# Two levels of seven products for the second pass's queries, over pairs of groups and both blocks

## The chip, the core and the metric

The kernel runs on one core of a Trainium2 chip. The metric is the time of one execution in device microseconds (us). The engines are PE (TensorE matmul; PEld is its load of weights), DVE (VectorE), ACT (ScalarE), POOL (GpSimd) and SP (SyncE, which here only issues DMAs). Each engine works its instructions off in the order of the program. Matmuls write PSUM; DVE and ACT read PSUM, POOL works on tiles in SBUF alone.

## What is computed

Two layers are applied to x of 8 x 256 tokens with 1024 channels, everything in float32:

```python
# layer 0: autocorrelation of layernorm(x) against ctx, times tanh(gate); then a linear layer with a
#          low-rank part whose rank is chosen by token
# layer 1, attention (the part that the change touches):
q = (layernorm(x) @ wq).reshape(B, S, 32, 128)     # 32 query heads
k = (ctx @ wk).reshape(B, S, 8, 128)               # 8 key heads, each serves a group of 4 query heads
v = (ctx @ wv).reshape(B, S, 8, 128)
q, k = rope(q), rope(k)
x = x + tanh(g) * (softmax(mask(q @ k.T / sqrt(128))) @ v) @ wo
# layer 1, a linear layer with folded low-rank parts
```

## The kernel before, in words

The 2048 tokens are worked off in two passes of 1024 tokens (`p` = 0, 1). Each pass has four stages, one after the other: `autocorrelation` with the keys and values beside it, `lora_ffn`, `attention`, `fourier_ffn`. A pass keeps its tokens in eight tiles `xt` of 128 tokens; four of them are a block, so a pass has two blocks of 512 tokens.

Nearly all large matrix products are done with seven products in place of eight (a 2 x 2 scheme of Strassen and Winograd): `left_operands` (L206) and `right_operands` (L215) make three sums and a difference of an operand's quarters, the products run in the order SEVEN = (1, 2, 6, 7, 4, 5, 3), and `combine` (L223) or `add_product` (L247) puts them together on DVE as they come. Stored sums of weights are written to memory in the first pass and loaded later.

`attention` goes over steps, one for each (block, group): all eight groups of block 0, then those of block 1. For a step:

- `load_wq` brings the seven operands of the group's query weights (512 KB each) two steps ahead, and `queries` (L967 to L978) runs seven products of 2 x 4 matmuls with 256 columns. `combine` takes seven DVE instructions for them. The four finished quarters, which still lie in PSUM, go through `rope` (L709 to L717): three DVE instructions and an add on POOL (L717). The scratch tile of `rope` has one buffer.
- `query_operands` makes the block's seven right-hand operands: a normalisation on DVE, 32 transposes on PE, copies on ACT, four sums on DVE. For block 0 this happens at the end of `lora_ffn`, for block 1 at step 6.
- `scores` is called four times a step, `values` one call behind. A score call is four matmuls (L1131), then masking and the maximum on DVE, exp and scaling on ACT; a value call is eight transposes (L1166) and four matmuls (L1177).
- The output projection follows. In the second pass (`paired`) it takes two steps together, `outputs_of_two` (L1015 onwards), in two levels of seven: 49 products of two matmuls with 256 columns (L1067). Its weights are streamed by `stream_wo`, seven tiles ahead; sums of the outer level's left operand are made on POOL (L1046, L1056, L1116, L1119). The first pass has written its finer weights with `finer_weights` (POOL, L921 to L924).

The queries and the projection are generators. Two tables in the code, `q_fill` and `o_fill`, say how many of their products are put around each of a step's four score calls, so that PE has work while DVE and ACT do the softmax. A scheduler then sets the final order of the instructions on each engine. Query products and output products share four PSUM buffers (`at_mm`), scores have two, transposes and values two. Every DMA is issued by SP, in order; an issue waits until its destination tile is free. The large tiles come from rings of seven buffers for each of three groups: the tiles of the normalised x ("xn"), `gq` and `go`.

Of the kernel before, what the change touches and what calls it, by code (L numbers as in the profile page):

```python
# [11 lines left out]
F32 = mybir.dt.float32  # L12
# [7 lines left out]
P = 128  # L20
# [26 lines left out]
def flamingo_kernel(ctx: ExitStack, tc: tile.TileContext, a: dict, out: bass.AP):  # L47
# [52 lines left out]


    wo2_d = [dram.tile([P, 7, 2, 2, 2, S], F32, name=f"wo2_d{i}") for i in range(N_KV // 2)]

    wk_d, wv_d = (
        [[dram.tile([P, KC * P], F32, name=f"{k}_d{u}_{i}") for i in range(4)] for u in range(2)]
# [3 lines left out]
    def big_tile(group, shape, name):  # L109
        return big.tile([P, *shape], F32, tag=group, name=name)  # L110
# [229 lines left out]
    def norm_stats(tiles):  # L340
# [10 lines left out]
        nc.vector.reciprocal(rstd[:, :n], rstd[:, :n])  # L351
        return mv, rstd

    def normed(dst, xt, mv, rstd, i):
        nc.vector.tensor_scalar(
            dst, xt, mv[:, i, 0:1], rstd[:, i : i + 1], ALU.subtract, ALU.mult
        )
# [25 lines left out]
    def autocorrelation(p, xt, pools, beside, late):  # L383
# [11 lines left out]

        def normalize(b0, b1):

            n = b1 - b0
            mv, rstd = norm_stats(xt[b0 * 2 : b1 * 2])
            lin = stats.tile([P, 2 * n, 2], F32, tag="lin", name="lin", bufs=2)  # L400
            nc.vector.tensor_copy(lin[:, :, 0], rstd[:, : 2 * n])
            nc.vector.scalar_tensor_tensor(
                lin[:, :, 1], mv[:, : 2 * n, 0], -1.0, rstd[:, : 2 * n], ALU.mult, ALU.mult
            )
            for b in range(n):
                norms[b0 + b] = lin[:, b * 2, :], lin[:, b * 2 + 1, :]

        def dft(*terms):
# [438 lines left out]

    def attention(p, xt, gq, go, keep, norms, xops, ahead):  # L850
        with (
            tc.tile_pool(name="at1", bufs=1, reuse_waits="tile") as w1,
# [5 lines left out]
            steps = [(blk, g) for blk in range(TT // NBT) for g in range(N_KV)]  # L858
            wq, wo, kv = {}, {}, {}
            paired = p == NPASS - 1  # L860

            def load_wq(step):
                blk, g = step
                if p == 0 and blk == 0:
                    q = [
                        [big_tile(gq, [2, KH, DH], f"wq_{i}{k}") for k in range(2)]
                        for i in range(2)
                    ]
                    for i, k in ((0, 0), (0, 1), (1, 0), (1, 1)):
                        nc.sync.dma_start(q[i][k], a["wq"][g, i, k])  # L870
                    s = [big_tile(gq, [2, KH, DH], f"wq_s{i}") for i in (1, 2, 4)]
                    ops = left_operands(nc.vector, q, *s)
                    for d, r in zip(wq_d[g], (5, 7, 6, 3)):
                        nc.sync.dma_start(d, ops[r])
                else:
                    ops = {}
                    where = {1: a["wq"][g, 0, 0], 2: a["wq"][g, 0, 1], 4: a["wq"][g, 1, 1]}
                    where |= dict(zip((5, 7, 6, 3), wq_d[g]))
                    for r in SEVEN:
                        ops[r] = big_tile(gq, [2, KH, DH], f"wq_{r}")  # L880
                        nc.sync.dma_start(ops[r], where[r])
                wq[step] = ops

            def load_wo(step):
                blk, g = step
# [43 lines left out]
            def stream_wo():  # L929

                places = []
                for _, g in steps[::2]:
                    for n, r in enumerate(SEVEN):
                        q = [
                            [wo_operand(g + k, r)[:, :, j * S : (j + 1) * S] for j in range(2)]
                            for k in range(2)
                        ]
                        d = wo2_d[g // 2][:, n]
                        places += [(q[0][0], q[1][0]), d[:, 0], d[:, 1], (q[1][1],)]
                tiles = []  # L940
                for n, src in enumerate(places):
                    for coming in places[len(tiles) : n + 7]:
                        tiles.append(big_tile(go, [2, 2, S], "wo"))
                        if isinstance(coming, tuple):
                            for i, part in enumerate(coming):
                                nc.sync.dma_start(tiles[-1][:, i], part)
                        else:
                            nc.sync.dma_start(tiles[-1], coming)
                    for i in range(len(src) if isinstance(src, tuple) else 2):
                        yield tiles[n][:, i]  # L950
# [16 lines left out]
            def queries(step, qT):  # L967

                wops, xo = wq[step], xops[step[0]]
                tiles = {}  # L970
                for r in SEVEN:
                    ps = ps_mm.tile([P, 2, S], F32, tag="mm", name="ps_q")
                    for l in range(2):
                        for c in range(KH):
                            nc.tensor.matmul(  # L975
                                ps[:, l, :],
                                wops[r][:, l, c, :],
                                xo[r][:, c, :],  # L978
                                start=(c == 0),
                                stop=(c == KH - 1),  # L980
                            )
                    done = combine(r, ps, tiles, lambda tag: half(tag, 1), lambda ps: ps)
                    if done:
                        qT[done[1]] = half("qT", 7)
                        rope(qT[done[1]], done[0], tab_q[:, 0, :], tab_q[:, 1, :], w1)
                    yield

            def outputs(step, ops):
                blk = step[0]
# [199 lines left out]
                    next(gen, None)  # L1189

            nothing = iter(())
            fine = nothing
            new_xl = lambda: big_tile("xn", [D], "xl")
            if paired:
                wo_stream = stream_wo()
            load_wq(steps[0])
            load_kv(steps[0])
            qT = {}
            for _ in queries(steps[0], qT):
                pass  # L1200
            norms[1] = norm_stats(xt[NBT:])
            load_wq(steps[1])
            last, before, o_gen = [], None, nothing
            end = len(steps) - 1

            if paired:
                q_fill = {0: (2, 2, 1, 1), 1: (2, 2, 2, 1), end: (0, 0, 0, 0)}
                o_fill = {k: (0, 5, 10, 10) if k % 2 == 0 else (3, 5, 8, 8) for k in range(end)}
                o_fill[end] = (6, 6, 6, 6)
            else:  # L1210
                q_fill = {0: (2, 2, 1, 1), end: (0, 0, 0, 0)}
                o_fill = {k: (0, 1, 3, 3) for k in range(end)}
                o_fill[end] = (2, 2, 2, 1)
            middle = 4 if paired else 1

            def start_outputs():
                if paired:
                    got = outputs_of_two(last[0][0][0], [oT for _, oT in last])
                else:
                    s = [half(f"oS{j}", 1) for j in (1, 2, 4)]  # L1220
# [3 lines left out]

            oT = [[None, None], [None, None]]
            for k, step in enumerate(steps):
                follow = k + 1 < len(steps)
                following = {}
                if follow:
                    load_kv(steps[k + 1])  # L1230
                    q_gen = queries(steps[k + 1], following)
                    if k == 0:
                        fill_from(q_gen, 1)
                else:
                    q_gen = nothing
                for i, (n, l) in enumerate(((0, 0), (0, 1), (1, 0), (1, 1))):
                    got = scores(step, l, n, qT)
                    nq = q_fill.get(k, (3, 3, 1, 0))[i]
                    no = o_fill[k][i]
                    fill_from(q_gen, nq)  # L1240
                    mid = min(no, middle)
                    if i > 0:
                        fill_from(o_gen, no - mid)
                    if before is not None:
                        values(*before, lambda: fill_from(o_gen, mid))
                    before = step, l, n, got, oT
                    if i == 0:
                        if len(last) == 1 + paired:
# [1 line left out]
                            fill_from(o_gen, no)  # L1250
                        else:
                            fill_from(o_gen, no - mid)
                    if i == 2 and k + 2 < len(steps):
                        if steps[k + 2][1] == 0:
                            blk = steps[k + 2][0]
                            xb = xt[blk * NBT : (blk + 1) * NBT]
# [3 lines left out]
                        load_wo(step)  # L1260
                    if i == 0 and p == 0 and step[0] > 0 and step[1] % 2:
                        fine = finer_weights(step)
                    fill_from(fine, 1)
                for _ in q_gen:
                    pass
                if not paired or k % 2:
                    for _ in o_gen:
                        pass
                last.append((step, oT))
                oT = [[None, None], [None, None]]  # L1270
                qT = following
            values(*before, lambda: None)
            o_gen = start_outputs()
            fill_from(o_gen, 14 if paired else 2)
# [73 lines left out]
    for p in range(NPASS):  # L1348
# [42 lines left out]
        with tc.tile_pool(name="at_keep", bufs=1, reuse_waits="tile") as kp:  # L1391
            keep, norms, xops = [], {}, {}

            def before_attention(pool, ps_t, tag):
                norms[0] = norm_stats(xt[:NBT])
                new = lambda: pool.tile([P, D], F32, tag="xn", name="xl")
                xops[0] = query_operands(xt[:NBT], norms[0], new, ps_t, tag)
                for b in range(BP):
                    mf = pool.tile([P, 2, S], F32, tag="mf", name="mf")
                    nc.sync.dma_start(mf, a["mask"][p * BP + b].rearrange("(i p) k -> p i k", p=P))  # L1400
# [171 lines left out]
```

## Time and profile before

Three runs took 3330.26, 3332.24 and 3340.0 us. The profiled execution was a fourth:

| | |
|---|---|
| its own time | 3340.92 us |
| span, first to last instruction | 3339.1 us |
| granted TensorE clock, mean | 0.992 |
| PE idle, whole span | 72 us |
| second pass's attention begins (first query) | 2212.9 us |
| its last score call | about 3175 us |
| matmuls of the queries, both passes (ps_q, L975) | 3584 records |
| memory traffic | 505.55 MB, 151 GB/s |
| longest wait for POOL by PE (before L1004, first pass's end) | 6.02 us |

The profile gives for each group of instructions its line, engine, operation, output and inputs, size, count, busy time and mean. A matmul of float32 appears as two records. Views by stage give the busy time of each engine in a stretch of the span. A view of waits gives who waited for whom; the chain goes back from the last instruction to what released it. "Idle before" is the time for which an engine stood still ahead of an instruction, with the instruction that ended it.

### The profile page before, as it was taken

Reading aid. Unit: us, or ns where it says so; the run is one execution under the profiler, and the core shown is the slowest. Engines: PE = TensorE matmul, PEld = TensorE weight load, DVE = VectorE, ACT = ScalarE, POOL = GpSimd, SP = SyncE. Lnnn points to the kernel's source line nnn. Section 1 sums busy time; section 2 is a strip of 40 time slices with the busy share of each in tenths; the row PEclk is TensorE's granted clock in tenths of the full one; section 3 lists DMA queues with packets and bytes.
Section 4 is the critical chain, followed back from the end, with each engine's and each line's share of the span. In section 5 each row is a group of like instructions: output and inputs, shape, how many; then the busy total and the mean of one; then the engine's idle time right before and its main releaser. Section 6 shows DMA issues by size and latency. Waiting matters only on the chain. (4 is left out here: it accounts for less than half of the span.)

```text
span 3339.1 us, 39371 instructions
## 1 busy us (share of the span) xinstructions
PE 3267.4 (98%) x13456; PEld 2405.0 (72%) x13456; DVE 2221.3 (67%) x4305; ACT 1051.6 (31%) x2555; POOL 1404.9 (42%) x1181
## 2 busy tenths in 40 slices
PE   8999899999999999999999999999999999999999
PEld 6677456777677777775456677568888888888874
DVE  7787657777776655565647686456666767666773
ACT  1332111433333433334113332115343434334420
POOL 4554111323332474576344442112454454454572
PEclk9999999999999999999999999999999999999999
DMA  7534615333433354554354435043555455555551
GB/s 280 175 115 125 235 65 186 130 134 129 145 124 130 132 208 145 183 195 162 115 190 130 138 117 171 7 158 101 168 175 167 160 167 172 166 168 176 171 192 51
DMA packets 215781, 505.55 MB, mean 151 GB/s; under 512 B 25076, under 2 KB 102900, under 8 KB 215582
## 3 DMA queue, kind: packets, MB, share of 16 engines
q1 hardware_dynamic: 214430, 498.84, 44.2%
q0 software_dynamic: 1152, 4.19, 0.3%
q8 instruction: 108, 1.77, 0.2%
q14 instruction: 91, 0.75, 0.1%
HBM read 394.96 MB, written 108.00 MB: 151 GB/s over the span
## 5 line engine op out<-in xcount | busy, mean ns | idle before, releaser
L717 POOL TENSOR_TENSOR qT<-qT,rope 128x512 f32<-128x512 f32 x128 | 170.1, 1329 | 789.9 <-DVE qT L716 750.8
L975 PE MATMUL ps_q<-xn,wq 128*128 128x256 f32 x1920 | 428.9, 379 | 0.0
L975 PEld LDWEIGHTS ps_q<-xn,wq 128*128 128x128 f32 x1920 | 364.8, 190 | 50.5 <-PE po L677 0.5
L1145 ACT ACTIVATE s<-s,nmx 128x256 f32<-128x256 f32 x512 | 255.9, 500 | 245.0 <-DVE nmx L1142 244.8
L1140 DVE COPY_PREDICATED s<-keep,ps_s 128x512 f32<-128x512 uint8 x256 | 184.8, 727 | 156.0 <-PE ps_s L1131 155.1
L975 PE MATMUL ps_q<-xn_t,wq 128*128 128x256 f32 x1280 | 285.6, 379 | 0.0
L370 DVE SCALAR_TENSOR_TENSOR x<-po,tg,x 128x512 f32<-128x512 f32 x248 | 177.3, 743 | 139.3 <-PE po L1319 44.7
L975 PEld LDWEIGHTS ps_q<-xn_t,wq 128*128 128x128 f32 x1280 | 243.2, 190 | 33.1
L1172 ACT COPY wT<-pt 128x512 f32<-128x512 f32 x256 | 138.8, 586 | 361.8 <-PE pt L1166 361.8
L1131 PE MATMUL ps_s<-kT,qT 128*128 128x256 f32 x1024 | 247.9, 379 | 0.0
L1177 PE MATMUL av<-wT,v 128*128 128x256 f32 x1024 | 246.0, 382 | 1.7 <-ACT wT L1172 1.6
L1154 ACT ACTIVATE s<-s,tot 128x256 f32<-128x256 f32 x512 | 230.1, 497 | 40.6 <-DVE tot L1152 40.5
L1177 PEld LDWEIGHTS av<-wT,v 128*128 128x128 f32 x1024 | 191.4, 190 | 54.8 <-issue 22.2
L1067 PE MATMUL po<-wo,oI 128*128 128x256 f32 x896 | 214.7, 379 | 2.0 <-issue 1.2
L1131 PEld LDWEIGHTS ps_s<-kT,qT 128*128 128x128 f32 x1024 | 191.8, 190 | 25.1 <-issue 0.5
L1004 PE MATMUL po<-wo,oT 128*128 128x512 f32 x448 | 201.6, 593 | 0.0
L1067 PEld LDWEIGHTS po<-wo,oI 128*128 128x128 f32 x896 | 168.7, 190 | 25.6 <-issue 2.0
L1185 ACT COPY oT<-av 128x512 f32<-128x512 f32 x128 | 75.0, 586 | 353.9 <-PE av L1177 352.4
L1142 DVE TENSOR_REDUCE nmx<-s 128x2 f32<-128x512 f32 x256 | 173.2, 682 | 6.9
L1067 PE MATMUL po<-wo,oT 128*128 128x256 f32 x672 | 172.1, 382 | 1.9 <-DVE co L1082 0.3
L253 POOL TENSOR_TENSOR x<-x,part 128x512 f32<-128x512 f32 x48 | 68.3, 1423 | 247.1 <-ACT part L252 247.1
L1004 PEld LDWEIGHTS po<-wo,oT 128*128 128x128 f32 x448 | 83.0, 191 | 83.2 <-issue 74.8
(290 smaller groups left out, 6407.1 us busy)
## 6 DMA issues: line engine op xcount, KB each, us to landing
wo<-wo_d SPq DMA_DIRECT2D x144, 512.0 KB, 4.6
wq<-in_wq_dram SPq DMA_DIRECT2D x104, 512.0 KB, 3.5
wq<-wq_d SPq DMA_DIRECT2D x96, 512.0 KB, 3.3
wo<-in_wo_dram SPq DMA_DIRECT2D x56, 512.0 KB, 3.5
wo_d<-fine_t SPq DMA_DIRECT2D x56, 512.0 KB, 3.4
wo<-wo_d SPq DMA_DIRECT2D x96, 256.0 KB, 3.4
w<-w_d SPq DMA_DIRECT2D x36, 512.0 KB, 5.3
wo<-in_wo_dram SPq DMA_DIRECT2D x72, 256.0 KB, 3.3
```

Source lines behind the costliest of these rows:

```text
L370: nc.vector.scalar_tensor_tensor(xs, ps, g, xs, ALU.mult, ALU.add)
L717: nc.gpsimd.tensor_add(dst, dst, t)
L975: nc.tensor.matmul(ps[:, l, :], wops[r][:, l, c, :], xo[r][:, c, :], start=(c == 0), stop=(c == KH - 1),)
L1004: nc.tensor.matmul(po, ops[r][:, h, t * P : (t + 1) * P], wops[r][:, h, :], start=(h == 0), stop=(h == 1),)
L1067: nc.tensor.matmul(po, left[r2][:, h, :], w[:, h, :], start=(h == 0), stop=(h == 1))
L1131: nc.tensor.matmul(ps[:, t, :], qT[i, n][:, l, t * P : (t + 1) * P], kT[:, n * S : (n + 1) * S], start=True, stop=True,)
L1140: nc.vector.copy_predicated(s, keep[b], ps)
L1142: nc.vector.tensor_reduce(nmx, s, AX.X, ALU.max, negate=True)
L1145: nc.scalar.activation(s[:, t, :], s[:, t, :], AF.Exp, bias=nmx[:, t : t + 1], accum_out=tot[:, t : t + 1],)
L1154: nc.scalar.activation(s[:, t, :], s[:, t, :], AF.Copy, scale=tot[:, t : t + 1])
L1172: nc.scalar.copy(wT[i], pt)
L1177: nc.tensor.matmul(av[:, i, :], kv[step][1][:, n * 2 + c, :], wT[i][:, c, :], start=(c == 0), stop=(c == 1),)
```

## The change

Only the queries of the second pass change in what is computed how; a step of preparation is added to the first pass.

**Second pass.** Seven products remain the inner level (`n`), and a second level of seven (`r1`) is laid over them. Its left operand is the weights of two groups, split by group and by half of the inner contraction; its right operand is the inner operands of both blocks. So all queries of two groups and two blocks, four steps, come from 49 products of 2 x 2 matmuls with 256 columns (`queries_of_all`), one generator for all pairs of groups. Each outer product is first combined from its seven inner ones, then its four quarters are combined among the outer ones by further DVE instructions; finished quarters go through `rope` as before.

The steps are in another order: for each pair of groups (block 0, g), (0, g+1), (1, g+1), (1, g). Both operands of a product are streamed by `load`, 256 KB each, seven products ahead. For the first two outer products (`m < 14`) the right operand is block 0's own tile.

`second_block` makes block 1's operands at the start of the attention rather than at step 6: normalisation on ACT, transposes on PE, copies on ACT, four sums on DVE, and then for the outer level 28 subtractions of 128x512 on POOL, whose results SP writes to memory (`x2_d`), where `load` fetches them. It runs beside the first 14 products.

**First pass.** `finer_queries` loads the inner operands of two groups, makes the four outer sums on POOL (4 x 7 subtractions or additions of 128x512 for each pair of groups, 112 in all) and writes them to memory (`wq2_d`). It runs beside block 0's steps, one part at each score call.

The tables `q_fill` and `o_fill` of the second pass are new, and one query product of each call is moved between the transposes and the matmuls of `values`.

In the built program PE has 7392 instructions where it had 7504, DVE 4310 (4113), ACT 2040 (2019), POOL 1319 (1179) and SP 1653 (1128).

```diff
+            if paired:
+                order = (0, 0), (0, 1), (1, 1), (1, 0)
+                steps = [(blk, g + i) for g in range(0, N_KV, 2) for blk, i in order]
...
+            def finer_queries(g):
...
+                coming = [load(0)[0]]
+                yield
+                for n in range(7):
+                    (q00, q01), (q10, q11) = coming[n]
+                    if n < 6:
+                        coming.append(load(n + 1)[0])
+                    nc.gpsimd.tensor_add(q11, q10, q11)
+                    nc.gpsimd.tensor_sub(q10, q00, q10)
+                    nc.gpsimd.tensor_sub(q00, q11, q00)
+                    nc.gpsimd.tensor_sub(q01, q01, q00)
+                    for i, q in enumerate((q00, q01, q10, q11)):
+                        nc.sync.dma_start(
+                            wq2_d[g // 2][:, n, i], q.rearrange("p l d -> p (l d)")
+                        )
+                    yield
...
+            def second_block(kept):
...
+                for u in range(4):
+                    norm(u)
+                    turned(u)
+                yield
+                lin.append(factors(xt[NBT + 2 : TT]))
+                norm(4)
+                norm(5)
+                yield
+                yield
+                for u in range(4, 8):
+                    if u % 2 == 0 and u < 6:
+                        norm(u + 2)
+                        norm(u + 3)
+                    turned(u)
+                    if u % 2:
+                        yield
+                sums = Steps(nc.vector)
+                s = [big_tile(go, [KH, S], f"xn_t{i}") for i in (1, 2, 4)]
+                ops = right_operands(sums, q, *s)
+                late = {}
+                for n, r in enumerate(SEVEN):
+                    if n < 4:
+                        sums.run((0, 2, 1, 3)[n])
+                    both = xops[0][r], ops[r]
+                    b = [x[:, k * KQ : (k + 1) * KQ, :] for k in range(2) for x in both]
+                    t1, t2 = (half("oT", 13) for _ in range(2))
+                    nc.gpsimd.tensor_sub(t1, b[1], b[0])
+                    nc.gpsimd.tensor_sub(t2, b[3], t1)
+                    flat = [t.rearrange("p b s -> p (b s)") for t in (t1, t2)]
+                    nc.sync.dma_start(x2_d[n][3][:, 0], flat[1])
+                    nc.sync.dma_start(x2_d[n][2][:, 0], flat[0])
+                    late[n] = b, t2
+                    kept[0] += 1
+                    yield
+                for n, r in enumerate(SEVEN):
+                    b, t2 = late[n]
+                    nc.gpsimd.tensor_sub(b[1], b[3], b[1])
+                    nc.sync.dma_start(x2_d[n][1], ops[r].rearrange("p (k c) s -> p k (c s)", k=2))
+                    nc.gpsimd.tensor_sub(t2, t2, b[2])
+                    nc.sync.dma_start(x2_d[n][4][:, 0], t2.rearrange("p b s -> p (b s)"))
...
+            def queries_of_all(kept, qT, places):
...
+                            while len(ops) < min(m + 7, kept[0]):
+                                load()
+                            w = ops[m][:, 0].rearrange("p (l c d) -> p l c d", l=2, c=KQ)
+                            if m < 14:
+                                k = m // 7
+                                x = xops[0][r][:, k * KQ : (k + 1) * KQ, :]
+                            else:
+                                x = ops[m][:, 1].rearrange("p (c s) -> p c s", c=KQ)
+                            m += 1
+                            ps = ps_mm.tile([P, 2, S], F32, tag="mm", name="ps_q")
+                            for l in range(2):
+                                for c in range(KQ):
+                                    nc.tensor.matmul(
+                                        ps[:, l, :],
+                                        w[:, l, c, :],
+                                        x[:, c, :],
+                                        start=(c == 0),
+                                        stop=(c == KQ - 1),
+                                    )
+                            at = {2: (0, 0), 5: (1, 1), 3: (0, 1), 4: (1, 0)}.get(r)
+                            dest = lambda ps: u1[at] if r1 == 1 else ps
+                            done = combine(r, ps, tiles, lambda tag: half(tag, 1), dest)
+                            if done and r1 != 1:
+                                u, w = u1[at], w1_[at] if r1 in (7, 4, 5) else None
+                                if r1 == 7:
+                                    nc.vector.tensor_add(w, ps, u)
+                                if r1 in (6, 5):
+                                    nc.vector.tensor_add(u, ps, u)
+                                if r1 == 4:
+                                    nc.vector.tensor_sub(ps, w, ps)
+                                if r1 in (2, 5, 3):
+                                    nc.vector.tensor_add(ps, ps, w if r1 == 5 else u)
+                                if r1 in (2, 4, 5, 3):
+                                    step = {2: (0, g), 4: (0, g + 1), 5: (1, g + 1), 3: (1, g)}[r1]
+                                    q = next(places["q"])
+                                    rope(q, ps, tab_q[:, 0, :], tab_q[:, 1, :], w1)
+                                    qT.setdefault(step, {})[at] = q
+                            yield
...
+                sums = second_block(kept)
+                next(sums)
+                for _ in range(14):
+                    next(q_gen)
+                    next(sums)
+                for _ in sums:
+                    pass
...
+                q_fill = {k: (3 + (k % 4 == 1), 3, 3, 3) for k in range(end)}
+                q_fill[0] = 6, 6, 6, 6
+                q_fill |= {end - 2: (2, 2, 2, 1), end - 1: (1, 1, 1, 1), end: (0, 0, 0, 0)}
+                o_fill = {k: (4, 7, 7, 7) if k % 2 == 0 else (6, 6, 6, 6) for k in range(end + 1)}
...
+                    late = paired and nq > 0
+                    fill_from(q_gen, nq - late)
+                    mid = min(no, middle - 2 * late)
```

## The prediction, made before the changed kernel had run

> **What bounds the kernel now.** I read the busy rows of the page first, then the busy time by stage, then the chain.
>
> ```profile
> PE 3267.4 (98%) x13456; PEld 2405.0 (72%) x13456; DVE 2221.3 (67%) x4305; ACT 1051.6 (31%) x2555; POOL 1404.9 (42%) x1181
> ```
>
> PE is busy for 98%, so only less PE work can bring much. By stage (us; busy time and instructions of PE, PEld, DVE, ACT, POOL; granted clock; DMA share; GB/s):
>
> ```profile
> 520.00:1000.00 480.00, 479.12 (x1958) 349.01 (x1957) 355.40 (x536) 168.43 (x446) 150.53 (x108) 1.00 0.41 145
> ...
> 2213.00:2340.00 127.00, 126.98 (x618) 110.61 (x617) 82.72 (x149) 54.68 (x150) 27.21 (x25) 1.00 0.37 120
> ...
> 2730.00:2860.00 130.00, 129.76 (x633) 113.68 (x631) 92.95 (x181) 51.94 (x136) 61.33 (x60) 1.00 0.52 170
> ```
>
> The second pass's attention begins at 2213. PE idles there for 0.24 us in 130, DVE has about 30% free, POOL half. Its opening, 2213 to 2340, has no idle PE at all. The chain, in order of time, is PE's own instructions:
>
> ```profile
> 2213.02 27.63 PE ps_q L975 x128
> 2242.38 6.91 PE ps_q L975 x32
> ```
>
> Those 128 records last 27.63 us: 0.2159 us a record, and an f32 matmul of 256 columns is two records (the program has 1792 such query matmuls, the page's L975 groups 3584 records), so 0.4317 us.
>
> **The saving.** Before, the second pass's queries are 16 steps x 7 products x 8 matmuls = 896. After, 4 pairs of groups x 49 products x 4 = 784. So 112 fewer x 0.4317 = 48.3 us of PE. The other PE work, the 32 transposes of the second block included, stays in number; the transposes move from the middle to the opening, where their stage had 0.4 us more idle PE than its neighbours.
>
> **DVE.** Two levels need more sums. The built program has 197 more DVE instructions, nearly all 128x512 reads of PSUM, at 0.69 us (L714 to L716, L244): +135 us. Spread over the stage's 920 us they fit (68% becomes about 86%), but they are uneven. By outer product, DVE does per seven inner products 7 ops (outer 1), 11 (6, 7), 23 (2, 4, 3) and 27 (5); the large ones end in four ropes of three ops. So 21 neighbouring products (4, 5, 3) bring 73 x 0.69 = 50.4 us. One score call with what is filled around it lasts 15.8 us before, 15.0 after, and takes 3.06 products. Its other DVE work is 88 us x 15.8/130 = 10.7 less 4.75 x 0.69 for its present queries = 7.4. The 21 products last 6.9 calls, 103 us: DVE 50.4 + 51 = 101.5. That is 98%; the light part of each pair is at 75%.
>
> Such a stretch has 12 ropes. Their scratch tile has one buffer, so L714 waits for POOL's add (L717) of the rope before: 1.33 us, against 1.4 us of sums between ropes. In the trace this wait is nothing, 0.7 us over 128 ropes; after, POOL may have one op of 0.75 (L1046) ahead. Bounds: 0 and about 1.4 us a rope. I take 0.5, near the trace's row: 6 us, less 1.5 spare and 1.5 that four PSUM buffers absorb: 3 a stretch, 12 in four stretches. ACT gains 12 copies of 0.59 and eight normalisations of 0.81 at 31% busy: nothing.
>
> **The opening.** The second block's operands are now made while the first 14 products run. POOL has 28 subtractions of 128x512 to do, and the rope's add stands behind them. In the built order the first rope's add comes after 23 of them, the second after 27; PE's first score waits for the first, its second half for the second. Rows: 128x512 on POOL takes 1.27 to 1.33 (L717, L921). Four can start as soon as ACT has copied two tiles; the fifth needs DVE's sum over all four tiles. That needs the last normalisation (factors wait for the residual at 2214.3, so four ACT ops of 0.8, two 0.59 copies, a 1.23 us sum), about 13.5 us after the first query. Then 19 x 1.30 + 1.33 puts the first rope's add at 39.5. PE gets there after 14 x 1.727 + 32 x 0.108 = 27.7, plus 1.3 for transposes that wait for ACT: 29.0. It waits 10.5 us. The next four and the second rope take 6.5; PE has 0.9 of work: 5.6 more. With 2 us for products whose PSUM buffer DVE, itself behind POOL's rope, has not freed: 19. Queued behind that PE wait are products 14 to 19, whose operands come through memory: SP writes each difference and reads it back (2.5 + 3.3 us by the landings), in 0.33 to 0.5 us an issue; SP waits for POOL's last subtraction at about 46, and the loads behind it land by 51, before PE needs them.
>
> A gap also costs clock. The trace has one of this kind, a 6.02 us wait for POOL in the first pass's end:
>
> ```profile
> 1590.12 3.78 PE L1004 MATMUL po<-wo,oS 128*128 128x512 f32 x4 [6.02 <-POOL oS L211]
> ```
> ```profile
> 1590.00:1600.00 10.00, 7.97 (x15) 3.95 (x16) 7.73 (x9) 1.17 (x2) 6.20 (x5) 0.50 0.34 130
> ```
>
> After it the granted clock is 0.50 for some 10 us, and eight 512-column records take 0.92 each instead of 0.43: about 5 us lost. The Trainium skill (TensorE: Matmul & The Clock Gate, What's actually happening) lets the array recover after about 3.4 us of activity, which would make it 1.7. The row decides: 5. The opening costs 24; bounds 17 (POOL at 1.27, clock by the rule) and 32.
>
> **DMA and SP.** 525 more issues, 0.33 to 0.5 us each, on an SP that mostly waits. Each product loads 512 KB, seven ahead, about 34 us before use; the rate in pass two goes from 170 to about 220 GB/s. Only the catch-up after the opening, 18 products in 31 us, asks 303 GB/s. The mix above moves 170 at a share of 0.52, so 327; pieces of 1 and 2 KB could do less. Bounds 0 and 6; I take 1.
>
> **First pass.** finer_queries adds 112 POOL ops x 1.3 = 147 us and 58 MB to the stage 520 to 1000: POOL 31% to 62%, DMA 0.41 to about 0.76. What it queues ahead of (POOL's operands for the outputs, SP's loads of weights) is needed a score call or a step later, 14 to 60 us. Here a rule speaks against the change: POOL shares its SBUF interfaces with DVE, and contends with DVE instructions of two SBUF inputs (GPSIMD Engine Reference, Key points). The trace agrees: the same L1094 add takes DVE
>
> ```profile
> 3128.53 1.80 DVE L1094 TENSOR_TENSOR x<-x,co 128x512 f32<-128x512 f32 x1
> ...
> 3130.84 0.69 DVE L1094 TENSOR_TENSOR x<-x,co 128x512 f32<-128x512 f32 x1
> ```
>
> The first stands beside POOL, and the stage's 64 operand sums of 128x1024 are of a kind that runs from 1.23 to 2.29 (L217 to L219 at 2188). By the rule all 64 would slow, +68 us; by the rows DVE then has 423 of 480, still under PE. So it costs PE nothing unless POOL holds back SP: bounds 0 and 8, I take 1.
>
> **Sum.** The profiled execution took 3340.92 for a span of 3339.1; the runs' median is 3332.24, and I subtract from that. 48.3 - 24 - 12 - 1 - 1 = 10.3 us saved: 3322.
>
> **Rivals.**
> The surplus is absorbed: POOL keeps to 1.27, the clock recovers by the rule, stretches lose 1 each. 48.3 - 18 - 4 - 1 = 25: 3307. For it: DVE's spans overlap in the trace (pitch 0.60 for 0.69).
> DVE becomes the bound, and the time is longer: in the stretch 4, 5, 3 each rope waits w for POOL; the loss is 12w - 3 a stretch. With the opening's 26 it passes the saving when w > 0.72 us. At 1.1 (an op of 0.75 in front of the add, less the sums between) the stretches lose 41: 3332 + 19 = 3351. For it: 98%, in-order queues on both; against: the 0.7 us in the trace.
> The first pass pays: SP waits for POOL's subtractions, weights come late, 10 us: 3331.
> That the matmuls aren't fewer is excluded by the built program.
>
> **Chances.** Forecast 0.42, reaching 3309 to 3336: 0.24 of it faster by over 0.3% (10 us, about what a measurement of this kernel tells from no change), 0.18 within. Absorbed 0.27, faster. DVE-bound 0.24, slower. First pass 0.07, 0.05 within and 0.02 slower. So 0.51, 0.23, 0.26. The range 3300 to 3352 leaves out the far ends of the second and third.
>
> **What would show it.** The query rows of pass two at 1568 records; PE idle of about 10 and 5 us waiting for qT by POOL some 29 us into the attention, with a clock of 0.5 behind it; DVE near 100% for some 100 us per pair, with short PE waits on DVE; the stage 520 to 1000 unchanged. I am wrong if the opening has no gap, if L714's successor waits a microsecond per rope, or if PE waits for q_ops.

## The result and the profile after

The changed kernel takes 3393.98 us (median of four runs, 3392.9 to 3397.78) where the kernel before takes 3334.19: a ratio of 1.0179, with a 95% interval of 1.0164 to 1.0194. The forecast was 3322, with a range to 3352. The change is slower, by 60 us.

The page's first part. PE does 21 us less work than before, and stands still for 150 us where it stood for 72:

```profile
PE 3246.0 (96%) x13232; PEld 2373.6 (70%) x13232; DVE 2346.1 (69%) x4502; ACT 1063.7 (31%) x2574; POOL 1582.9 (47%) x1321
```

Where the time went is read from the places where stages begin (us, from each trace):

| | before | after | difference |
|---|---|---|---|
| first query of pass one's attention | 542.3 | 541.7 | |
| from there to the first product of `fourier_ffn` | 1072.7 | 1134.0 | **+61.3** |
| from there to the first query of pass two's attention | 597.9 | 600.4 | +2.5 |
| from there to the end | 1126.2 | 1119.9 | **-6.3** |

So the second pass gained, as forecast, though less (10.3 + 1 for the first pass: 11.3 were expected, 6.3 came). The loss is in the first pass, where the forecast had put 1 us. PE has the same work there in both kernels; of the 61.3 us, 44.8 are time in which it stands idle (55.3 for 10.5), and 16.5 are the same work taking longer (1078.7 us busy for 1062.2) at a granted clock of 0.974 for 0.994. Busy time by stage (columns as before: length, then PE, PEld, DVE, ACT, POOL, granted clock, DMA share, GB/s):

```profile
520.00:1000.00 480.00, 437.87 (x1716) 315.73 (x1715) 326.08 (x476) 143.95 (x384) 273.17 (x196) 0.96 0.70 241
...
2730.00:2860.00 130.00, 128.85 (x626) 113.01 (x626) 105.07 (x195) 53.24 (x142) 60.34 (x61) 1.00 0.68 217
```

In the first row PE is idle for 42 us where it was idle for 0.9, and the clock falls to 0.96. DVE, POOL and DMA are all below 75%: nothing is full, so it is waiting, not work. Who waits for whom, 541 to 1080 (total, times, longest; `po <- qT` is an output product that waits for a PSUM buffer which the ropes still read):

```profile
PE po L1207 <- DVE qT L729: 26.2, 7, 8.3
PE ps_q L1034 <- DVE qT L729: 12.6, 3, 6.9
```
```profile
DVE wq_s L217 <- DMA wq<-in_wq_dram: 36.6, 5, 14.0
DVE rope L727 <- POOL qT L730: 23.7, 7, 5.4
```
```profile
SPq L937 <- POOL fine_q L934: 82.3, 21, 7.3
...
SPq L920 <- DMA wq_d<-fine_q: 25.0, 16, 3.3
SPq L937 <- POOL fine_q L935: 16.4, 13, 2.7
SPq L937 <- POOL fine_q L933: 16.2, 3, 7.9
...
SPq L937 <- POOL fine_q L932: 5.5, 1, 5.5
```

PE waits for DVE, which is 68% busy. DVE waits for two things that it did not wait for before: the raw query weights (L217) and POOL's add of the rope before (L727). SyncE stands 120 us at the stores of the finer weights (L937), whose sums POOL has not made yet, and 25 us at their loads (L920), whose tile has not been stored yet. One such place, by engine:

```profile
714.20 10.07 SPq L937 DMA_DIRECT2D wq_d<-fine_q  x5
724.36 0.38 SPq L890 DMA_DIRECT2D wq<-in_wq_dram  x1
```
```profile
716.90 0.70 DVE L250 TENSOR_TENSOR ps_q<-w,ps_q 128x512 f32<-128x512 f32 x1 [2.69 <-PE ps_q L1034]
728.86 1.23 DVE L217 TENSOR_TENSOR wq_s<-wq,wq 128x1024 f32<-128x1024 f32 x1 [11.26 <-DMA wq<-in_wq_dram]
730.12 0.69 DVE L727 TENSOR_TENSOR rope<-ps_q,tab_q 64x512 f32<-64x512 f32 x1
```
```profile
732.27 6.16 PE L1034 MATMUL ps_q<-xn,wq_s 128*128 128x256 f32 x16 [4.18 <-DVE qT L729]
```

Five stores occupy SyncE for 10 us. The last quarter of raw weights is issued behind them, at 724.4. DVE stands at its sum for 11.3 us, with the rope's operations, which need none of it, behind. PE runs out of work, and its next 16 records take 6.16 us where 3.5 would do (16 x 0.2159): the granted clock is 0.5 until 737.2. Behind each of the seven gaps of over 2 us that PE has from 541 to 1080 it is 0.5 for another 2.9 to 5.5 us.

What put POOL's sums there is the order of the built program; the traces have POOL's instructions in the same order. Around the first score calls of the stage, as the scheduler set it ("f" a sum of the finer weights, "R" a rope's add, "." another operation, "|" a score call on PE):

```
before             .......RRR|RR||R|R|RR|....R.R.|R......||R|....R.R.|
after              .....RffffffRffR|RR|ffff|ffffRfff|fR|ffffRffffR|....fffffRfff.R.|
sums held in order .......RRR|RR||R|R|RR|....ffffR.R.ff|ffR......|ffffffff|R|
```

The code starts `finer_queries` at the fourth score call. In the built program six sums stand in front of a rope's add before the first call. Why the scheduler puts them there was not looked into.

The second pass, on the other hand, went much as written. Its opening:

```profile
2276.00:2313.00 37.00, 30.24 (x145) 25.26 (x143) 24.08 (x33) 8.37 (x15) 25.07 (x18) 0.92 0.48 156
2313.00:2353.00 40.00, 27.08 (x116) 22.49 (x117) 25.90 (x48) 15.38 (x42) 17.46 (x15) 0.77 0.66 244
2353.00:2403.00 50.00, 48.66 (x232) 42.10 (x231) 40.93 (x68) 13.12 (x36) 7.61 (x6) 1.00 0.92 313
2403.00:2470.00 67.00, 65.73 (x324) 56.49 (x323) 58.60 (x111) 35.44 (x95) 32.96 (x33) 1.00 0.70 229
```
```profile
2320.63 2.07 PE L1334 MATMUL ps_s<-kT,qT 128*128 128x256 f32 x4 [12.23 <-POOL qT L730]
2326.75 2.07 PE L1334 MATMUL ps_s<-kT,qT 128*128 128x256 f32 x4 [4.04 <-POOL qT L730]
```

The two waits for the ropes' adds are there, 12.23 and 4.04 us (10.5 and 5.6 forecast), and the granted clock is 0.77 in the 40 us that hold them.

### The profile page after: what moved, and what is told of

Read it like the earlier page. It is cut to its first block, busy times and chain, and to the rows that moved or that the text cites. A ratio compares the mean times of both kernels' runs of the same rounds, so it can differ in the third digit from the quotient of the medians.

```text
span 3396.0 us, 40329 instructions
## 1 busy us (share of the span) xinstructions
PE 3246.0 (96%) x13232; PEld 2373.6 (70%) x13232; DVE 2346.1 (69%) x4502; ACT 1063.7 (31%) x2574; POOL 1582.9 (47%) x1321
## 5 line engine op out<-in xcount | busy, mean ns | idle before, releaser
L1164 PE MATMUL ps_q<-q_ops 128*128 128x256 f32 x1456 | 336.0, 381 | 1.4 <-DMA q_ops<-x_d 0.7
L730 POOL TENSOR_TENSOR qT<-qT,rope 128x512 f32<-128x512 f32 x99 | 130.2, 1315 | 371.2 <-DVE qT L729 347.0
L1164 PEld LDWEIGHTS ps_q<-q_ops 128*128 128x128 f32 x1456 | 273.2, 191 | 39.2 <-issue 2.4
L1334 PE MATMUL ps_s<-kT,qT 128*128 128x256 f32 x792 | 195.2, 383 | 19.1 <-POOL qT L730 16.3
L1034 PE MATMUL ps_q<-xn,wq 128*128 128x256 f32 x896 | 200.1, 379 | 0.0
L1034 PEld LDWEIGHTS ps_q<-xn,wq 128*128 128x128 f32 x896 | 170.2, 190 | 23.6 <-PE po L690 0.2
L1334 PEld LDWEIGHTS ps_s<-kT,qT 128*128 128x128 f32 x792 | 149.8, 192 | 41.1 <-POOL qT L730 17.4
L1369 PEld LDWEIGHTS pt<-ident,s 128*128 128x128 f32 x1024 | 122.7, 142 | 31.4 <-issue 18.0
```

The costliest lines, as they stand in the source:

```text
L1034: nc.tensor.matmul(ps[:, l, :], wops[r][:, l, c, :], xo[r][:, c, :], start=(c == 0), stop=(c == KH - 1),)
L1164: nc.tensor.matmul(ps[:, l, :], w[:, l, c, :], x[:, c, :], start=(c == 0), stop=(c == KQ - 1),)
L1334: nc.tensor.matmul(ps[:, t, :], qT[i, n][:, l, t * P : (t + 1) * P], kT[:, n * S : (n + 1) * S], start=True, stop=True,)
L1369: nc.tensor.transpose(pt[:, c, t * P : (t + 1) * P], got[i][:, t, c * P : (c + 1) * P], ident,)
```

## The experiments

Times are device us; "attention 1" is the stretch of the table above that had become 61.3 us longer. Where no interval is given, a run is one execution (about 0.3%), and the stretches of its trace say more than its time: beside these runs the kernel before took from 3331 to 3344 us.

| run | attention 1 | pass two's attention to end | time |
|---|---|---|---|
| before | 1072.7 | 1126.2 | 3334.2 |
| after | 1134.0 | 1119.9 | 3394.0 |
| finer weights left out | 1071.2 | 1117.8 | 3331.9 |
| transfers alone | 1083.8 | 1119.2 | 3343.2 |
| sums alone | 1182.2 | 1116.2 | 3432.3 |
| sums alone, held in order | 1077.2 | 1116.6 | 3328.7 |
| stores from POOL's queue | 1167.9 | 1116.2 | 3426.8 |
| sums held in order | 1110.4 | 1119.4 | 3370.1 |
| sums, loads, stores held in order | 1114.2 | 1119.6 | 3375.0 |
| sums on DVE | 1107.5 | 1114.6 | 3358.5 |
| loads and stores on ACT's queue | 1076.0 | 1115.4 | 3333.6 |
| stores on ACT's, loads on SP's | 1076.9 | 1122.0 | 3332.0 |
| opening held in order | 1131.6 | 1102.7 | 3367.9 |
| both repairs | 1076.1 | 1103.3 | 3319.1 |

The stretch between the two lasts 597 to 600 us in some runs and 590 to 591 in others (the one before lies at 597.9, the one with both repairs at 591.2). One DVE instruction, in a stage that no edit touches, decides it: it lasts 6.62 us in the eight traces of the first kind and 1.74 in the six of the second, and PE behind it waits 6.3 to 6.7 us, or 1.4 to 1.8. Before, and with both repairs:

```profile
1898.18 6.62 DVE L466 SCALAR_TENSOR_TENSOR ke<-end,ke 128x512 f32<-128x512 f32 x1 [7.97 <-POOL ke L460]
```
```profile
1902.92 1.74 DVE L479 SCALAR_TENSOR_TENSOR ke<-end,ke 128x512 f32<-128x512 f32 x1 [7.97 <-POOL ke L473]
```

So the stretches are compared, where it matters, without it.

**Without the finer weights.**

```diff
-                        fine_q = finer_queries(k)
+                        fine_q = nothing
```

> The finer query weights of the first pass are neither loaded, made nor stored; the second pass reads other stored weights of the same shape in their place, so the queries of the second pass are not the reference's. My theory (the first pass's making of them costs the 61.3 us by which the first pass's attention became longer, 1072.7 to 1134.0 us): that attention is back at 1073 (within 3), and the time is about 3394 - 62 = 3332, the second pass's 6 us gain counted in. Rival (the second pass, not the first, holds most of the loss, or the streamed loads of the second pass slow everything): 3370 or more.

3331.85 us, a ratio to before of 0.9979 (0.9971 to 0.9986); attention 1 is 1071.2. All of the loss belongs to `finer_queries`; against the kernel before, which took 3338.5 beside it, what is left is a small gain.

**Its transfers alone, its sums alone.**

```diff
-                    nc.gpsimd.tensor_add(q11, q10, q11)
...
-                    nc.gpsimd.tensor_sub(q01, q01, q00)
```

> GpSimd's 112 sums are left out; every load and store of the finer query weights stays, so what is stored is the unsummed operands. Theory (SyncE's in-order queue stands at the stores until GpSimd has summed, and the raw weights behind them come late): the wait on GpSimd is gone, the traffic (some 240 GB/s in the stage) is the same, the first pass's attention falls to 1073 to 1090, the time to 3332 to 3350. Rival (the traffic itself delays the raw weights): the attention stays at 1115 or more, the time above 3375. Half and half: about 3360.

```diff
-                    (q00, q01), (q10, q11) = coming[n]
-                    if n < 6:
-                        coming.append(load(n + 1)[0])
+                    (q00, q01), (q10, q11) = coming[0]
...
-                    for i, q in enumerate((q00, q01, q10, q11)):
-                        nc.sync.dma_start(
-                            wq2_d[g // 2][:, n, i], q.rearrange("p l d -> p (l d)")
-                        )
```

> GpSimd's 112 sums stay, on tiles that are loaded once for each pair of groups; the other loads and all stores of the finer weights are left out, and the second pass reads other stored weights. Theory (GpSimd's work by itself is harmless, only SyncE's waits for it cost): attention of the first pass 1073 to 1080, time 3332 to 3340. Rival (the sums stand ahead of the ropes' adds on GpSimd, VectorE waits for those and PE for VectorE: the waits of VectorE on GpSimd, 23.7 us, stay): 3350 to 3360.

The transfers alone cost 12.6 us (1083.8 less 1071.2), at up to 325 GB/s in a stretch of 60 us, more than after's 300. So bandwidth by itself is not the 61 us; at most it is these 12.6. The sums alone, with nothing to store, cost 111 us, more than everything together: the theory that they are harmless fell, and its rival (3350 to 3360) was far too low. DVE's waits, sums alone:

```profile
DVE rope L727 <- POOL qT L730: 103.8, 8, 33.5
```

In the built order all 112 sums now stand in front of the tenth of the stage's rope adds, up to 24 between two; with the loads in place they had reached to the thirtieth, up to 15 between two. The trace has the last sum at 740 us; with the order held (below) it ends at 1136. The transfers thus shield the kernel from its own sums, and the parts do not add up.

**Stores from POOL's own queue.** POOL knows when its sums are done, so SyncE is spared the wait.

```diff
-                        nc.sync.dma_start(
+                        nc.gpsimd.dma_start(
```

> Everything is computed; the stores of the finer query weights are issued from GpSimd's own queue behind the sums that they store, so SyncE no longer waits there for GpSimd. Theory (SyncE's wait is the cause): VectorE's 38 us of waits for the raw weights fall under 10, the first pass's attention to 1075 to 1095, the time to 3335 to 3355; what GpSimd pays for issuing 112 stores is not known, 1 us each would be 112 us on an engine that is 57% busy in the stage and could bring the ropes' waits up. Rival (traffic): 3375 or more, as before the edit.

Missed: 3426.8. The issues last 0.557 us each, 63 us in all, on the engine whose queue was the trouble, and nothing became of the raw weights, because the loads on SyncE still wait for the stores to have landed (139.8 us at L920):

```profile
DVE wq_s L217 <- DMA wq<-in_wq_dram: 40.2, 4, 13.7
...
DVE rope L727 <- POOL qT L730: 25.4, 6, 6.6
```

These two waits are about as long as in the changed kernel, whose stage is 34 us shorter. What is new are five of DVE's 128x1024 sums, which last 5.8 to 9.7 us in place of 1.22, 31 us too long together. PE's two longest gaps stand behind the two longest of them:

```profile
746.39 9.70 DVE L217 TENSOR_TENSOR wq_s<-wq,wq 128x1024 f32<-128x1024 f32 x1 [13.74 <-DMA wq<-in_wq_dram]
```
```profile
758.27 2.07 PE L1034 MATMUL ps_q<-xn,wq_s 128*128 128x256 f32 x4 [15.14 <-DVE qT L729]
```

In these 9.70 us POOL works without a break, on seven additions and subtractions of 128x512 one behind the other and its issues. No run separates this from the rest.

**The order held.** Each sum is queued behind what stands before it in the code on its engine; this is an order, not a wait.

```diff
-                    nc.gpsimd.tensor_add(q11, q10, q11)
+                    tc.keep_in_program_order(nc.gpsimd.tensor_add(q11, q10, q11))
```

> As the run with the sums alone (tiles loaded once for a pair, no stores, other stored weights read in the second pass), which lost 100 us, but each sum is held behind what stands before it in the code on GpSimd. It tells GpSimd's order from GpSimd's work (its 147 us, its contention with VectorE). If the order is the cause: the first pass's attention within 5 us of the 1071 without any of this, the time 3330 to 3338. If the work is: still 1130 or more, time above 3385.

Sums alone, in order: attention 1 falls from 1182.2 to 1077.2. The same 112 sums cost 6 us over the kernel without finer weights (1 us more than expected). Their place costs 105 us, their work hardly anything. What PE still waits for:

```profile
PE po L1203 <- DVE qT L729: 5.8, 5, 1.2
```

With the transfers back:

> The run with the sums alone cost 100 us, the one with the transfers alone 12 us over the one with neither. So my theory is now: the scheduler puts GpSimd's sums far ahead of their place in the code, up to ten in front of a rope's add; VectorE stands at the rope's scratch tile and PE behind VectorE. Here each of the 112 sums is held behind all that stands before it in the code on GpSimd (an order, no wait); nothing else is changed. Theory: VectorE's waits on GpSimd in the first pass (23.7 us) fall under 5, the first pass's attention to 1080 to 1095 us (12 of transfers stay), the time to 3340 to 3355. Rival (SyncE's stores, which wait for the sums, hold the raw weights back; later sums make that worse): VectorE's waits for raw weights stay at 30 us or more, time 3375 or more.

Half right. DVE's wait for POOL is gone from the list, and attention 1 is 24 us shorter, but 39 of 63 remain:

```profile
DVE wq_s L217 <- DMA wq<-in_wq_dram: 24.0, 6, 5.6
```
```profile
SPq L937 <- POOL fine_q L932: 135.4, 21, 9.3
...
SPq L937 <- POOL fine_q L934: 28.3, 23, 4.0
SPq L937 <- POOL fine_q L935: 27.1, 20, 1.8
...
SPq L937 <- POOL fine_q L933: 20.4, 21, 1.5
```

SyncE now stands 211 us at the stores where it stood 120: the rival's mechanism is real too.

> As the run with the sums held in the order of the code, and the loads and stores of the finer query weights are held in it on SyncE too. Theory (order on GpSimd is most of it, SyncE's order the rest): time 3335 to 3350. If SyncE's place matters more than GpSimd's: clearly (15 us or more) below the run that holds the sums alone. If it doesn't matter: the same within 5 us.

Holding SyncE's issues in the code's order as well gave nothing (1114.2). SyncE stands only 31 us at the stores, and DVE's wait for raw weights falls to 5.2 us; but its wait for POOL at the ropes is back, 34.0 us. The reason: the loads of the finer weights now stand behind loads that wait for PE, come late, and POOL stands at them, with a rope's add behind.

```profile
POOL fine_q L932 <- DMA fine_q<-wq_d: 70.8, 8, 23.4
POOL fine_q L932 <- DMA fine_q<-in_wq_dram: 66.6, 5, 20.0
```

**The sums on DVE**, placed by the scheduler:

> The 112 sums run on VectorE in place of GpSimd, 112 x 0.69 = 77 us more on an engine that is busy 326 of 480 us in the stage; the scheduler places them. Theory (GpSimd's order is the cause): the waits on GpSimd are gone; what VectorE loses to its own sums ahead of ropes is half as long a sum and without a hand-over: first pass's attention 1085 to 1105, time 3345 to 3365. Rival (VectorE then stands itself at the sums' loads): 3380 or more.

3358.5, attention 1 1107.5, 2.5 us over the expected range. POOL is out of it, and still 36 us are lost: DVE stands at the sums' loads itself (11.3 us), SyncE at stores that wait for DVE. So a faster engine does not cure it: DVE's queue gets waits of the same kind.

**SyncE spared.** The transfers move to ACT's queue, a product's stores half a score call behind its sums, the next loads half a call behind those; a tile is loaded by one DMA in place of two. The sums are held in order.

```diff
+                for n in range(8):
+                    if n:
+                        store(n - 1, coming[n - 1])
+                    yield
+                    if 0 < n < 6:
+                        coming.append(load(n + 1))
...
+                    yield
```

> Everything is computed. The finer query weights' loads and stores leave SyncE for ScalarE's queue, held in the order of the code; a product's stores are issued half a score call after its sums and its tiles are loaded again half a call after that, so that no issue should stand; one load a tile in place of two; the sums are held in order on GpSimd. The three parts so far add up as 24 us (GpSimd's order), 12 (the transfers), the remaining 27 (SyncE at the stores). If that is right: no VectorE waits for raw weights over 3 us, first pass's attention 1075 to 1090, time 3335 to 3350. Rival (the transfers' bandwidth holds the raw weights back wherever they are issued): 1100 or more, 3360 or more. ScalarE's issues, some 192 at 0.5 us, could hold its copies back: bounds 0 and 15.

> As the run with both on ScalarE's queue, but the loads stay on SyncE where the scheduler puts them; stores on ScalarE's. If SyncE's waits for GpSimd at the stores were the harm: as good as that run within 5 us. If loads that wait on SyncE for their tile to be stored are harmful too: 10 us or more above it.

Both do it: attention 1 is 1076.0 and 1076.9, 5 to 6 us above the kernel without the finer weights, with all transfers and sums in it. DVE has no wait left for raw weights or for ropes' adds, but for one of 0.6 us in the second. In the first the granted clock of the stage (520 to 1000) is 1.00, and PE's waits from 541 to 1100 are small:

```profile
PE av L1390 <- ACT wT L1385: 2.4, 4, 0.6
PE po L1217 <- DVE x L389: 1.1, 1, 1.1
```

In the second, SyncE still stands at loads whose tile has not been stored yet (127.5 us), to no harm. Which of the three edits (queue, half a call's distance, fewer issues) is needed was not taken apart, nor whether a second DMA queue helps by itself.

**The opening of pass two.** The 28 subtractions of `second_block` are held in order; the rest is the changed kernel. In the built order 8 of them stand before the first rope's add, where 23 did.

```diff
-                    nc.gpsimd.tensor_sub(t1, b[1], b[0])
+                    tc.keep_in_program_order(nc.gpsimd.tensor_sub(t1, b[1], b[0]))
...
```

> Only the second pass's opening differs from the changed kernel: the 28 subtractions of the second block are held in the order of the code on GpSimd, so that few stand ahead of the first rope's adds. The first pass keeps its loss. My prediction priced the opening at 24 us, 16 of them PE's waits for GpSimd (measured 12.23 + 4.04) and 5 of clock. By that: both waits gone, time lower by 12 to 21, 3373 to 3382. Rival (the differences are needed through memory by products 14 on, and are now later): PE waits for q_ops in place of the rope, time 3388 to 3400.

Pass two's attention to the end is 17.2 us shorter (1119.9 to 1102.7): PE's idle time falls by 12, its busy time, for the same work, by 5 (of which the stage's opening has 3.6, by the granted clock; 1.7 belong to a place at 3263 that the edit does not touch). Of the waits for POOL one of 4.6 is left:

```profile
2297.94 2.08 PE L1334 MATMUL ps_s<-kT,qT 128*128 128x256 f32 x4 [4.59 <-POOL qT L730]
```

The rival's new wait, for operands through memory (q_ops from x2_d), is 1.1 us. The time, 3367.9, is below the 3373 expected because the stretch between the passes was at 589.7 us in this run.

**Both repairs.**

> The two repairs together, everything computed: finer query weights loaded and stored from ScalarE's queue with the sums held in order, and the second block's 28 subtractions held in order on GpSimd. If the two places are independent, 3333.6 less the 17 us that the opening's repair gave (second pass's attention to end 1119.9 to 1102.7): 3316, and against the kernel before a ratio of about 0.994. If the opening's gain came only because the kernel was late elsewhere: 3330 to 3335, a ratio of 0.998 to 1.000.

3319.14 us, median of six, against 3331.27 for the kernel before: 0.9959 (0.9944 to 0.9974). This version computes everything and beats both kernels. Its first-pass stage, beside the row of after above:

```profile
520.00:1000.00 480.00, 478.18 (x1949) 347.90 (x1948) 365.43 (x534) 167.63 (x444) 281.09 (x192) 1.00 0.69 234
```

POOL and DMA carry the same load (281 and 273 us, 234 and 241 GB/s), and PE is full. The median's gain of 12 us is less than the 25.6 between the two profiled executions (spans of 3313.5 and 3339.1): the one lies at the fast end of its runs (3312.74 to 3322.48), the other at the slow end of its own, and 6.7 of the 25.6 are the stretch between the passes, which the repairs do not touch.

## Why the prediction was wrong, point by point

**The saving, 48.3 us: right.** The page has 1456 records on streamed operands, and 112 more run on block 0's own tile, 1568 as forecast. PE's busy time from pass two's first query to the end fell by 37.2, not 48.3. 6.7 of the 11 us were lost at a clock of 0.5 (5.0 in the opening, 1.7 at 3263); the rest, some 4 us, was not looked into.

**The opening, 24 (17 to 32): right in mechanism and size.** PE's idle time in the 194 us from the first query is 22.3 us, before 0.2 in as long a stretch. With the 5.0 us of clock that makes 27. PE came to the first wait after some 32 us, not 29.0. The repair of the opening gave 12 of the idle time and 3.6 of the clock back.

The 5 for the clock came true with a reading that does not hold in general. The row it was taken from, 0.50 over 10 us, has a second gap in it:

```profile
1595.81 1.94 PE L365 MATMUL pt<-ident,xn 128*128 128x128 f32 x8 [1.91 <-DVE xn L355]
```

Where no second gap follows closely, the clock was back within 6.2 us of a gap's end in every trace here, and often after 3. The figure of the Trainium skill (TensorE: Matmul & The Clock Gate, What's actually happening), 3.4 us of activity, was nearer for one gap than the row. But the opening too has two gaps, 12.23 and 4.04 us, and the clock is 0.50 from 2310.8 to 2331.3, with PE busy for 6.6 us of that after the first wait: 3.3 us lost there, and 1.7 at 2287, behind a gap of 2.1 us which the forecast did not have. That the sum is 5 again is in part luck.

**The heavy stretches, 12: too high.** In the steady 743 us from 2470 PE idles 8.2 us in all where it idled 1.8: 6.4. DVE takes 102 to 109 of 130 us, 78 to 83%; the forecast had 86%, though 135 us over the 920 that it names, on top of 68%, are 83%. Its fullest 100 us have 92.7 us of work, where 101.5 of 103 had been forecast, and it waits there for a rope's add 0.8 us in all. The rival in which DVE becomes the bound did not occur.

**DMA's catch-up, 1: right.** PE's waits for q_ops are 2.0 us in all; the catch-up ran at 313 GB/s.

**The first pass, 1 (0 to 8): the step that failed.** The prediction wrote: "So it costs PE nothing unless POOL holds back SP: bounds 0 and 8, I take 1." It cost 61.3. The step had three faults.
- It weighed the work (POOL at 62%, DMA at 0.76, DVE at 423 of 480 by the rows), and the work is nearly free: 112 sums in order cost 6 us, all transfers and sums off SyncE 5. Even the contention on which it spent a paragraph is small: with the transfers on ACT's queue DVE's operand sums of 128x1024 take 5 us more for the query weights and some 10 for the output weights than without the finer weights, not 68.
- It took the distance from the code: what the sums queue ahead of "is needed a score call or a step later". In the built program up to 15 of them stand between two ropes' adds, and the trace has DVE waiting for such an add seven times, up to 5.4 us, with PE waiting for DVE in turn. The prediction had counted such places for the opening, where it was right, and not for the first pass.
- It named the condition, "unless POOL holds back SP", and gave it a bound of 8 without a row. A store that waits for a sum stops everything behind it on SyncE; DVE waits up to 14.0 us for raw weights, and PE in turn for DVE. The third rival had this mechanism, at 10 us and a chance of 0.07.

Shown: the loss is `finer_queries`' (1071.2 without it); POOL's order is enough for a loss of 105 us, and holding it gives 24 of the 63 us back in the full kernel; the rest goes when the transfers leave SyncE and stand clear of the sums. Argued only: how much of after's 61 us each of the two was, since they feed each other (late sums make late stores, late loads make late sums).

## What to carry to other kernels

A step that is "beside" other work is priced by what its instructions stand in front of on each in-order queue, in the built order and not in the code's: count the instructions ahead of the next one that the bounding engine needs, and do it at every place that the change touches. An issue of a store that waits for a fresh result belongs on a queue where nothing urgent is behind it, or half a step later. When nothing in a stage is full and it has become slower, look at who waits for whom; then hold an order, before anything is made faster or moved to another engine.

## What the runs showed of the hardware

- A short gap costs more than itself. In the fourteen traces, behind gaps of PE of 2.1 to 17.9 us with no further one close behind, the granted clock was back at full 2.8 to 6.2 us after the gap's end, wherever it had fallen; it was at 0.5 after every such gap of over 3.7 us, and after some of those from 2.1 to 3.7. At 732.3, 16 records took 6.16 us, 0.385 each in place of 0.2159.
- Traffic of 325 GB/s over 60 us (DMA share 0.95) can pass beside PE-bound work without lengthening it: in the run with the transfers alone PE was busy for 59.86 of the 60 us from 780. In another such stretch, at 323 GB/s from 600, it idled 5 us.
- An issue of a store on POOL's queue took 0.557 us, on SyncE's 0.431 (medians of 112).
- POOL, busy for 280 of 480 us beside DVE, slowed DVE's two-input sums of 128x1024 less than expected: the 28 in the trace on the query weights take 45.4 us with the transfers on ACT's queue, 40.0 without the finer weights; those on the output weights 1.51 us each (31) and 1.20 (32).
- But a single one can be held up for long. Where POOL's operations followed one another without a break, a DVE instruction with two inputs in SBUF lasted up to 9.70 us in place of 1.22. The one of 6.62 us at 1898.18 ended 0.55 us after the last of five POOL operations in a row; in the six runs in which it took 1.74, a POOL operation beside it took 1.71 or 1.72 in place of some 1.26. Both outcomes come from the same order of POOL's and of DVE's instructions there.
